# Scan inputs built by TensorE instead of VectorE in a two-layer attention, MLP, Mamba and LoRA-expert kernel

## The chip, the cores and the metric

The kernel runs on one NeuronCore of a Trainium2 chip. The metric is the device time of one execution in microseconds (us). Before the change it is 840.49 us, the median of 3 runs (839.77 to 840.96).

## The reference

The input is x of 4 sequences by 256 tokens by 512 channels, in float32. Layer 0 adds a latent attention and a gated MLP to x; the change doesn't touch it. Layer 1 adds a selective scan (Mamba) and a mixture of low-rank experts on a dense base. Cut to what matters here, for each sequence:

```python
proj = xn @ in_proj_w                       # 512 -> 2 x 1024
x, z = split(proj)                          # both [1024, 256]
xc = silu(conv_b + sum_k conv_w[:, k] * shift(x, k))        # 4 taps
ssm = xc.T @ x_proj_w.T                     # 32 + 16 + 16 columns
dt_r, B, C = rmsnorm of the three parts
dt = softplus(dt_r @ dt_proj_w.T + dt_bias)                 # [1024, 256]
h[d, n, t] = exp(dt[d, t] * A[d, n]) * h[d, n, t-1] + dt[d, t] * B[n, t] * xc[d, t]
ys[d, t] = sum over the 16 n of h[d, n, t] * C[n, t]
y = (ys + D * xc) * silu(z)
out = y.T @ out_proj_w.T  (+ x + the experts)
```

The recurrence runs over 256 times for 4 sequences x 1024 channels d x 16 states n.

## The kernel before, in words

All work is written out by hand in program order for five engines; nothing is scheduled by a planner. Layer 0 comes first, with the last blocks of its MLP (`ff`, the generator `down`) trickling into the beginning of layer 1.

Layer 1 is a loop over 128 units `u` (L1377), 32 for each sequence: `b` is the sequence, `c` one of 8 blocks of 128 channels, `g` one of 4 groups of states. A tile of a unit has 128 partitions = 4 states x 32 channels, and a free dimension of 4 channel quarters x 256 times, 1024 in all. For each unit:

- `decays` (L969), ScalarE: four exponentials of 255 columns give exp(dt*A). It runs two units ahead.
- `scan_in` (L983), VectorE: one multiplication of 1024 columns, `bx` = a row of B (`brow`, in PSUM) times `dus`, where `dus` is dt*x laid out over 32-channel quarters. It writes PSUM, one buffer of two banks.
- `scan` (L991): VectorE's scan instruction over 1024 columns gives `h`; then GpSimd multiplies it by the row of C into `hc`.
- `states_sum` (L1012), TensorE: four float32 matmuls with 32 output columns each, one for each quarter of the output partitions, add `hc` into `ysum`. At a block's first unit a matmul with a diagonal of D (`dgs`, L1016) opens the sum.

To get from 128 channels in partitions to 32 channels x 4 states, dt and dt*x are written to DRAM (`send`, L931) and read back four times over (`spread`, L935), for each block, by SyncE's queue. `take_sum` (L1021) and `gate` (L1025) close a block, and `out_mm` (L1113) projects it.

Around these, a table (`put` and its kin, L1241 to L1373) places the other work at certain units: the input projections `px_mm` and `pz_mm`, the convolution (`conv_in`, `conv_taps`), `pp_mm` to `pp_norm`, the step sizes, and the dense and expert parts. Softplus is taken apart into Abs, Relu, Exp, two Identity and Ln on ScalarE (`step_in`, `step_exp`) and three GpSimd additions (`step_out`). Silu of z runs in several sessions a sequence (`gate_silu`, L951), each with a load of an activation table before and after. [...]3 for `psmm`, which nearly every matmul group draws on, 2 for `bx`, 1 for `ysum`, 2 for `brow`.

Of the kernel before, what the change touches and what calls it, by code (L numbers as in the profile page):

```python
# [8 lines left out]
F32 = mybir.dt.float32  # L9
# [8 lines left out]
P = 128  # L18
# [10 lines left out]
NG = 4  # L29
# [12 lines left out]
def block_kernel(  # L42
# [604 lines left out]
    psx = ctx.enter_context(tc.tile_pool(name="psx", bufs=1, space=PSUM))  # L647
    psy = ctx.enter_context(tc.tile_pool(name="psy", bufs=1, space=PSUM))
    psb = ctx.enter_context(tc.tile_pool(name="psb", bufs=1, space=PSUM))
# [6 lines left out]
    xcs, nrms, dts, szs, crows = {}, {}, {}, {}, {}  # L656


    al = w1.tile([P, NG, DC, NST], F32, tag="u", name="al")

    def load_rest():
# [14 lines left out]
    bcsel = w1.tile([64, 2, NU, P], F32, name="bcsel")  # L676
    nc.vector.tensor_copy(
        bcsel.rearrange("p k g (n j) -> p (k g n) j", n=NG),
        ident[0:64, RK : RK + 2 * NST].unsqueeze(2).to_broadcast([64, 2 * NST, NB]),
    )  # L680
    nc.vector.tensor_reduce(stack, ident.rearrange("p (n j) -> p j n", n=NG), AX.X, ALU.add)
    dgs = w1.tile([P, DC, P], F32, name="dgs")
# [17 lines left out]
    brow = [psb.tile([P, 2, S], F32, name=f"brow{i}") for i in range(2)]  # L700
# [15 lines left out]
    def norm_stats(b):  # L716
        mv = w1.tile([P, 2, 2], F32, tag="mv1", name="mv1", bufs=2)
        for i in range(2):
            st = w1.tile([P, 6], F32, tag="st1", name="st1", bufs=2)
            nc.vector.bn_stats(st, x[:, 2 * b + i, :])  # L720
            nc.vector.bn_aggr(mv[:, i, :], st)
        rs = w1.tile([P, 2], F32, tag="rsn", name="rsn", bufs=2)
        inv_root(rs, mv[:, :, 1], eps[:, 0:1])
        live["ln", b] = mv, rs

    def norm_scale(b):
        mv, rs = live["ln", b]
        sh = w1.tile([P, 2], F32, tag="sh1", name="sh1", bufs=2)
        nc.vector.scalar_tensor_tensor(sh, mv[:, :, 0], -1.0, rs, ALU.mult, ALU.mult)
        out = []  # L730
        for i in range(2):
            t = w1.tile([P, D], F32, tag="xnt", name="xnt", bufs=2)
            nc.scalar.activation(t, x[:, 2 * b + i, :], AF.Identity, bias=sh[:, i : i + 1],
                                 scale=rs[:, i : i + 1])
            out.append(t)
# [25 lines left out]
    both = ((1, 0), (1, 3), (2, 1), (2, 3), (3, 1), (3, 3))  # L761

    def conv_in(b, p):
# [5 lines left out]
        nc.scalar.copy(pads[p % 2][:, :, KC - 1 :], px)  # L769
        v = [vec[:, 2 * p + i, :] for i in range(2)]  # L770
        if b:
            dg = live["dg"] = w1.tile([P, KC, P], F32, tag="dg", name="dg")
            for k in range(KC):
                nc.scalar.activation(dg[:, k, :], ident, AF.Identity, scale=v[0][:, V_CW + k : V_CW + k + 1])
        tp = live["tap"] = w1.tile([P, KC - 1, S], F32, tag="tap", name="tap")
        if (b, p) in both:
            tp = tp.rearrange("p k t -> p (k t)")
            for k in range(KC):
                nc.scalar.activation(tp[:, k * P : (k + 1) * P], ident, AF.Identity,
                                     scale=v[1][:, V_CW + k : V_CW + k + 1])  # L780
        else:
            nc.scalar.activation(xcs[b][:, 2 * p + 1, :], px[:, 1, :], AF.Identity,
                                 bias=v[1][:, V_CB : V_CB + 1], scale=v[1][:, V_CW + KC - 1 : V_CW + KC])
            for k in range(KC - 1):
                nc.scalar.activation(tp[:, k, :], pads[p % 2][:, 1, k : k + S], AF.Identity,
                                     scale=v[1][:, V_CW + k : V_CW + k + 1])
        if b == 0:
            nc.scalar.activation(px[:, 0, :], px[:, 0, :], AF.Identity, bias=v[0][:, V_CB : V_CB + 1],
                                 scale=v[0][:, V_CW + KC - 1 : V_CW + KC])

    def conv_taps(b, p):
        px, c = live["px", b, p], 2 * p
        if b == 0:
            for k in range(KC - 1):
                nc.vector.scalar_tensor_tensor(
                    px[:, 0, :] if k < KC - 2 else xcs[b][:, c, :], pads[p % 2][:, 0, k : k + S],
                    vec[:, c, V_CW + k : V_CW + k + 1], px[:, 0, :], ALU.mult, ALU.add,
                )
        else:

            for i in range(1 + ((b, p) in both)):
                for k in range(KC):
                    dg = live["tap"].rearrange("p k t -> p (k t)")[:, k * P : (k + 1) * P]
                    mm(px[:, i, :], lhsT=dg if i else live["dg"][:, k, :],  # L804
                       rhs=pads[p % 2][:, i, k : k + S], start=(k == 0), stop=(k == KC - 1))
            if p < NP - 1:
                conv_out(b, p)
        if (b, p) not in both:
            xc = xcs[b][:, c + 1, :]
            for k in range(KC - 1):  # L810
                nc.gpsimd.tensor_tensor(xc, xc, live["tap"][:, k, :], ALU.add)

    def conv_out(b, p):
        for i in range(1 + ((b, p) in both)):
            c = 2 * p + i
            nc.scalar.activation(xcs[b][:, c, :], live["px", b, p][:, i, :], AF.Identity,
                                 bias=vec[:, c, V_CB : V_CB + 1])

    def conv_silu(b, z=None):
        nc.scalar.activation(xcs[b], xcs[b], AF.Silu)  # L820
        if z is not None:
            gate_silu(*z)
        else:
            exp_set()
# [9 lines left out]
    def pp_square(b):  # L834
        pp = live["pp"]
        sq = w1.tile([64, S], F32, tag="sq", name="sq")
        nc.scalar.activation(sq, pp[:64, 0, :], AF.Square)
        mm(pp[:64, 1, :], lhsT=cst[:64, C_BLK : C_BLK + 64], rhs=sq, start=True, stop=True)
        live["rs"] = w1.tile([64, S], F32, tag="sq", name="rs1")
# [9 lines left out]
    def b_rows(b, i):  # L849

        for g in (2 * i, 2 * i + 1):
            mm(brow[i][:, g % 2, :], lhsT=bcsel[:, 0, g, :], rhs=nrms[b], start=True, stop=True)

    def c_rows(b, i):
        pc = psmm.tile([P, 2, S], F32, tag="mm", name="pcr")
        for j in range(2):
            mm(pc[:, j, :], lhsT=bcsel[:, 1, 2 * i + j, :], rhs=nrms[b], start=True, stop=True)
# [5 lines left out]
    def step_in(b, h, q, part=(0, 1)):  # L863
        if q == 0 and part[0] == 0:
            dts[b, h] = odd(h).tile([P, HALF, S], F32, tag="dt", name="dt")
            live["u"] = w1.tile([P, HALF, S], F32, tag="u", name="u")
        pd = psmm.tile([P, 2, S], F32, tag="mm", name="pdt")
        for i in part:
            c = h * HALF + 2 * q + i
            mm(pd[:, i, :], lhsT=dtw[:, c * P : (c + 1) * P], rhs=nrms[b][0:RK, :],  # L870
               start=True, stop=True)
        for i in part:
            j = 2 * q + i
            db = vec[:, h * HALF + j, V_DB : V_DB + 1]
            nc.scalar.activation(live["u"][:, j, :], pd[:, i, :], AF.Abs, bias=db)
            nc.scalar.activation(dts[b, h][:, j, :], pd[:, i, :], AF.Relu, bias=db)

    def step_exp(b, h, q=slice(0, 4)):

        if q.start == 0:  # L880
            live["lw"] = w1.tile([P, HALF, S], F32, tag="lw", name="lw")
            live["e"] = w1.tile([P, HALF, S], F32, tag="e", name="e")
        u, w, e = (live[n][:, q, :] for n in ("u", "lw", "e"))
        nc.scalar.activation(u, u, AF.Exp, scale=-1.0)
        nc.scalar.activation(w, u, AF.Identity, bias=1.0)
        nc.scalar.activation(e, w, AF.Identity, bias=eps[:, 2:3])
        nc.scalar.activation(w, w, AF.Ln)


    def one_step(c):  # L890
        pd = psmm.tile([P, 2, S], F32, tag="mm", name="pdt")[:, 0, :]
        mm(pd, lhsT=dtw[:, c * P : (c + 1) * P], rhs=nrms[0][0:RK, :], start=True, stop=True)
        t = live["one"] = w1.tile([P, KC - 1, S], F32, tag="tap", name="one")
        u, w, e = (t[:, k, :] for k in range(3))
        db = vec[:, c, V_DB : V_DB + 1]
        nc.scalar.activation(u, pd, AF.Abs, bias=db)
        nc.scalar.activation(dts[0, 0][:, c, :], pd, AF.Relu, bias=db)
        nc.scalar.activation(u, u, AF.Exp, scale=-1.0)
        nc.scalar.activation(w, u, AF.Identity, bias=1.0)
        nc.scalar.activation(e, w, AF.Identity, bias=eps[:, 2:3])  # L900
        nc.scalar.activation(w, w, AF.Ln)

    def one_out(c):
        u, w, e = (live["one"][:, k, :] for k in range(3))
        dt = dts[0, 0][:, c, :]
        nc.gpsimd.tensor_tensor(e, u, e, ALU.subtract)
        nc.gpsimd.tensor_tensor(e, e, w, ALU.add)
        nc.gpsimd.tensor_tensor(dt, dt, e, ALU.add)

    def step_out(b, h, q, k):  # L910
        s = slice(2 * q, 2 * q + 2)
        e, dt = live["e"][:, s, :], dts[b, h][:, s, :]
        if k == 0:
            nc.gpsimd.tensor_tensor(e, live["u"][:, s, :], e, ALU.subtract)
        elif k == 1:
            nc.gpsimd.tensor_tensor(e, e, live["lw"][:, s, :], ALU.add)
        else:
            nc.gpsimd.tensor_tensor(dt, dt, e, ALU.add)
            send("dt", b, 2 * h + q, dt)

    def step_x(b, p):

# [608 lines left out]
```

## Time and profile before

The profile is of one execution, whose span is 839.1 us; the median of the runs is 1.4 us more.

| | us |
|---|---|
| median of the runs | 840.49 |
| span of the profiled execution | 839.1 |
| first scan input (L986) starts | 327.45 |
| last scan (L1001) starts | 830.3 |
| from the one to the other (the scan stage) | 502.8 |
| busy over the whole span: TensorE, VectorE, ScalarE, GpSimd | 748.8, 655.1, 554.7, 496.7 |

A group row names line, engine and operation, then output and inputs with their shapes, the count, the busy time, the mean duration of one in ns, and the idle time of the engine just before. For a tiled matmul, `128*32` is rows by columns of the array in use. A float32 matmul appears as two MATMUL and two LDWEIGHTS records, so that the four matmuls of `states_sum` are eight of each.

### The profile page before, as it was taken

To read this page: it belongs to the slowest core of one execution; us is meant where nothing else is said; L and a number is where in the kernel's file an instruction comes from. 1 tells how busy PE (TensorE), PEld (TensorE's weight loads), DVE (VectorE), ACT (ScalarE), POOL (GpSimd) and SP (SyncE) were. 2 spreads that over 40 slices of the span, in tenths; PEclk is the share of its full clock that TensorE was granted. 3 is DMA by queue.
4 is the path that set the end of the run, shared out by engine and by line. 5 is a ranking of instruction groups with operands and counts; after the bars stand their busy time and mean duration, and the time that the engine had idled before them with its cause. 6 is when DMAs were issued, how large, how long until landed. Compare 5 with 4: busy or idle time off the path is not lost.

```text
span 839.1 us, 11113 instructions
## 1 busy us (share of the span) xinstructions
PE 748.8 (89%) x3846; PEld 429.7 (51%) x3846; DVE 655.1 (78%) x604; ACT 554.7 (66%) x1124; POOL 496.7 (59%) x389
## 2 busy tenths in 40 slices
PE   4999999999999999999887899888999987956885
PEld 2665545666555676666543457444457444312331
DVE  4486756288634435798899999989999989999996
ACT  4335564435556277699896898687898786865561
POOL 3133332001343333688869799769699769798764
PEclk9799999999999999999999999989999989998998
DMA  7233332001222332554593554443553343343400
GB/s 226 63 101 105 97 101 62 1 1 38 76 76 80 114 57 64 151 140 125 137 215 114 150 155 125 110 103 117 144 164 114 88 113 111 103 125 102 113 26 25
DMA packets 68642, 86.71 MB, mean 103 GB/s; under 512 B 12221, under 2 KB 52169, under 8 KB 68458
## 3 DMA queue, kind: packets, MB, share of 16 engines
q1 hardware_dynamic: 58794, 65.81, 29.3%
q0 software_dynamic: 9072, 18.35, 7.9%
q10 hardware_dynamic: 720, 1.84, 0.6%
q8 instruction: 30, 0.49, 0.2%
q14 instruction: 26, 0.21, 0.1%
HBM read 66.58 MB, written 10.22 MB: 92 GB/s over the span
## 4 chain that ended last, share of the span: by engine, by line
PE 51%; DVE 25%; ACT 15%; POOL 5%; issue 3%; DMA 1%; DVEq 0%; POOLq 0%; ACTq 0%; SPq 0%
DVE h L1001 15%; ACT decay L980 7%; PE pg L444 6%; PE pu L444 5%; PE po L469 5%; PE px L757 4%; DVE bx L986 4%; POOL hc L1006 4%; PE av L397 4%; PE px L804 4%; PE ysum L1018 3%; PE scT L386 2%; DVE mpl L354 2%; PE pp L831 2%; PE po L1114 2%
## 5 line engine op out<-in xcount | busy, mean ns | idle before, releaser
L1006 POOL TENSOR_TENSOR hc<-h,cr 128x1024 f32<-128x1024 f32 (+1 forms) x130 | 301.7, 2323 | 79.9 <-DVE h L1001 67.5
L1001 DVE TENSOR_TENSOR_SCAN h<-decay,bx 128x1024 f32<-128x1024 f32 (+1 forms) x129 | 288.2, 2236 | 27.0 <-POOL hc L1006 4.7
L980 ACT ACTIVATE decay<-dts,aneg 128x255 f32<-128x255 f32 x504 | 213.4, 501 | 52.3 <-DVE h L1001 42.2
L986 DVE TENSOR_TENSOR bx<-brow,dus 128x1024 f32<-128x1024 f32 x128 | 157.7, 1232 | 5.0 <-DMA dus<-dud 0.6
L1018 PE MATMUL ysum<-hc,stack 128*32 128x256 f32 x1024 | 89.6, 419 | 42.2 <-POOL hc L1006 41.9
L456 POOL TENSOR_TENSOR hlo<-g,hhi 128x512 fp32r<-128x512 f32 x28 | 35.8, 1280 | 115.0 <-ACT hhi L455 115.0
L354 DVE TENSOR_REDUCE mpl<-sc 128x4 f32<-128x1024 f32 x64 | 76.7, 1219 | 22.8 <-PE sc L352 21.3
L427 POOL DMA_DIRECT2D wgu<-in_wgu x56 | 31.1, 555 | 95.9 <-PE pg L444 94.7
L388 ACT ACTIVATE pe<-scT 128x1024 f32<-128x1024 f32 x64 | 64.0, 1023 | 22.9 <-PE sc L352 14.3
L1114 PE MATMUL po<-ow,xc 128*128 128x512 f32 x128 | 69.4, 646 | 4.3 <-POOL xc L1026 3.9
L1018 PEld LDWEIGHTS ysum<-hc,stack 128*32 128x32 f32 x1024 | 21.3, 111 | 100.3 <-POOL hc L1006 70.6
L948 PE MATMUL pz<-xn1T,w_in 128*128 128x256 f32 x256 | 69.4, 420 | 0.0
L948 PEld LDWEIGHTS pz<-xn1T,w_in 128*128 128x128 f32 x256 | 50.8, 208 | 20.7 <-issue 11.9
L757 PE MATMUL px<-xn1T,w_in 128*128 128x256 f32 x256 | 60.9, 383 | 0.4 <-ACT sz L954 0.3
L757 PEld LDWEIGHTS px<-xn1T,w_in 128*128 128x128 f32 x256 | 47.6, 190 | 13.0 <-issue 2.5
L452 DVE SCALAR_TENSOR_TENSOR g<-g,pg 128x512 f32<-128x512 f32 x28 | 19.2, 686 | 43.1 <-ACT g L451 43.1
L444 PE MATMUL pg<-xhi,wgu 128*128 128x512 f32 x112 | 49.6, 443 | 1.0 <-ACT xhi L244 1.0
L469 PE MATMUL po<-wd,hhi 128*128 128x512 f32 x112 | 49.2, 439 | 0.0
L444 PE MATMUL pu<-xhi,wgu 128*128 128x512 f32 x112 | 47.6, 425 | 0.8 <-DVE g L454 0.8
L455 ACT CAST hhi<-g 128x512 fp32r<-128x512 f32 x28 | 17.3, 619 | 45.8 <-DVE g L454 45.8
L444 PE MATMUL pg<-xlo,wgu 128*128 128x512 f32 x112 | 44.9, 401 | 0.7 <-DVE xlo L251 0.7
L444 PE MATMUL pu<-xlo,wgu 128*128 128x512 f32 x112 | 44.5, 397 | 0.0
(237 smaller groups left out, 1276.8 us busy)
## 6 DMA issues: line engine op xcount, KB each, us to landing
dts<-dtd SPq DMA_DIRECT2D x124, 128.0 KB, 2.8
dus<-dud SPq DMA_DIRECT2D x124, 128.0 KB, 3.2
wgu<-in_wgu POOLq DMA_DIRECT2D x56, 256.0 KB, 2.7
w_in<-in_inz SPq DMA_DIRECT2D x16, 512.0 KB, 4.9
w_in<-in_inx SPq DMA_DIRECT2D x14, 512.0 KB, 4.3
dtd<-dt SPq DMA_DIRECT2D x15, 256.0 KB, 2.2
dud<-du SPq DMA_DIRECT2D x15, 256.0 KB, 2.2
wd<-in_wd POOLq DMA_DIRECT2D x7, 512.0 KB, 3.6
```

Of the source, the lines that this page charges most:

```text
L354: nc.vector.tensor_reduce(mpl2[b % 2][:, qb, 2 * hp : 2 * hp + 2, 16 + 2 * gq : 18 + 2 * gq], sc.rearrange("p i (f k) -> p i f k", f=2), A ...
L388: nc.scalar.activation(pes[b, k][:, 2 * t : 2 * t + 2, :], sc, AF.Exp)
L444: mm(ps, lhsT=wgus[i][:, hc, :], rhs=xs[j][:, hc, :], start=(hc == 0 and j == 0), stop=(hc == HC - 1 and j == 1))
L469: mm(po, lhsT=hids[th][j][:, m, i * P : (i + 1) * P], rhs=wd[:, m, :], start=False, stop=(m == MC - 1 and j == 1))
L757: mm(px[:, i, :], lhsT=w[:, i, hc, :], rhs=xns[b][:, hc, :], start=(hc == 0), stop=(hc == HC - 1))
L948: mm(pz[:, i, :], lhsT=w[:, i, hc, :], rhs=xns[b][:, hc, :], start=(hc == 0), stop=(hc == HC - 1))
L980: nc.scalar.activation(da[:, k, 1:], live["dts", b, c][:, k, 1:], AF.Exp, scale=aneg[:, c, k, g : g + 1])
L986: nc.vector.tensor_tensor(bx, brow[g // 2][:, g % 2, :].unsqueeze(1).to_broadcast([P, NG, S]), live["dus", b, c], ALU.mult)
L1001: nc.vector.tensor_tensor_scan(h[:, n].rearrange("p n t -> p (n t)"), da[:, n].rearrange("p n t -> p (n t)"), bx[:, n].rearrange("p n t -> ...
L1006: (nc.vector if k == NG - 1 else nc.gpsimd).tensor_tensor(hc[:, n], h[:, n], crows[b][:, g, :].unsqueeze(1).to_broadcast([P, NG // parts, ...
L1018: mm(ysum[k * NB : (k + 1) * NB, :], lhsT=stack, rhs=hc[:, k, :], start=False, stop=(g == NU - 1))
L1114: mm(live["po", b, i], lhsT=xcs[b][:, c, i * P : (i + 1) * P], rhs=late_w["ow"][:, c, :], start=False, stop=(c == DC - 1))
```

## The change

- `scan_in` is taken from VectorE and given to TensorE. `bx` becomes the product of a transposed dt*x (`dut`, made by `step_turn`) and diagonals of B (`bdg`, made by `b_turn` and `b_diag` once a sequence): 32 float32 matmuls a unit, each with 64 contraction rows, 32 output columns and 128 moving columns. `bx` gets two buffers, and the input of unit u+1 is issued at the start of unit u. The round trip of dt*x through DRAM is gone; that of dt stays.
- The order of the scans changes: a unit is now one quarter `k` of the channels with all four groups of states, so that the multiplication with C reads the whole of `crows`.
- `states_sum` sums four units at once, 16 matmuls after each fourth unit. D*x is added by VectorE in `take_sum`, and `dgs` is gone.
- Softplus is one ScalarE pass, for a whole sequence at once, between two table loads (`softplus_set`, `exp_set`). Silu of xc and z is one session a sequence (`silus`); z waits for it as a copy.
- The convolution uses other engines for some blocks: by `mode`, TensorE with diagonals that GpSimd makes once and DRAM keeps, ScalarE and GpSimd, or VectorE.
- `brow` is gone, so PSUM is 3 banks `psmm`, 4 `bx`, 1 `ysum`. One of the two accumulators `po` is closed into x and opened again by a matmul (`close_x`, `reopen`). The table of units is rewritten, and more tiles share buffers.

```diff
-    psx = ctx.enter_context(tc.tile_pool(name="psx", bufs=1, space=PSUM))
+    psx = ctx.enter_context(tc.tile_pool(name="psx", bufs=2, space=PSUM))
-    psb = ctx.enter_context(tc.tile_pool(name="psb", bufs=1, space=PSUM))
...
+    def mode(b, p, i):
+
+        if b == 0:
+            return "dve" if i == 0 else "act"
+        return "pe" if i == 0 else "act" if p < 2 else "dve"
...
+    def silus(b, z):
+
+        nc.scalar.preload_act_table_set("silu_and_others")
+        if b < B:
+            nc.scalar.activation(xcs[b], xcs[b], AF.Silu)
+        nc.scalar.activation(szs[z], szs[z], AF.Silu)
+        exp_set()
...
+    def b_turn(b):
+
+        bt = live["bt"] = psmm.tile([P, 4, 8], F32, tag="mm", name="pbt")
+        for t in range(4):
+            for r in range(2):
+                mm(bt[r * HT : (r + 1) * HT, t, :], lhsT=nrms[b][:, t * HT : (t + 1) * HT],
+                   rhs=ident[0:64, RK + 8 * r : RK + 8 * r + 8], start=True, stop=True)
+
+    def b_diag():
+
+        for i in range(2):
+            nc.vector.tensor_tensor(
+                bdg[:, 2 * i : 2 * i + 2].rearrange("p t g n j -> p (t g n) j"),
+                eye.unsqueeze(1).to_broadcast([P, NST, HT]),
+                live["bt"][:, 2 * i : 2 * i + 2, :].rearrange("p t s -> p (t s)").unsqueeze(2)
+                .to_broadcast([P, NST, HT]), ALU.mult,
+            )
...
+    def step(b, p):
...
+            nc.scalar.activation(dts[b][:, c, :], pd[:, i, :], AF.Softplus, bias=vec[:, c, V_DB : V_DB + 1])
...
+    def step_x(b, c, eng=nc.gpsimd):
+
+        live["du", c] = w1.tile([P, S], F32, tag="du", name="du", bufs=2)
+        eng.tensor_tensor(live["du", c], dts[b][:, c, :], xcs[b][:, c, :], ALU.mult)
+
+    def step_turn(b, c):
+
+        du = live["du", c]
+        pt = psmm.tile([P, 4, P], F32, tag="mm", name="ptu")
+        for t in range(4):
+            for r in range(2):
+                mm(pt[r * HT : (r + 1) * HT, t, :], lhsT=du[:, t * HT : (t + 1) * HT], rhs=ident,
+                   start=True, stop=True)
+        dut[b, c] = w1.tile([P, 4, P], F32, tag="dut", name="dut", bufs=2)
+        nc.scalar.copy(dut[b, c], pt)
...
     def scan_in(u):
-        b, c, g = u // PER, u % PER // NU, u % NU
-        bx = psx.tile([P, NG, S], F32, tag="bx", name="bx")
-        nc.vector.tensor_tensor(
-            bx, brow[g // 2][:, g % 2, :].unsqueeze(1).to_broadcast([P, NG, S]), live["dus", b, c], ALU.mult
-        )
-        live["bx"] = bx
+        b, c, k = u // PER, u % PER // NU, u % NU
+        bx = live["bx", u] = psx.tile([P, NU, S], F32, tag="bx", name="bx")
+        for t in range(4):
+            for n in range(NG):
+                for r in range(2):
+                    w = slice(r * HT, (r + 1) * HT)
+                    mm(bx[n * NB : (n + 1) * NB, 2 * r : 2 * r + 2, t * HT : (t + 1) * HT],
+                       lhsT=dut[b, c][w, t, k * NB : (k + 1) * NB], rhs=bdg[w, t, :, n, :],
+                       start=True, stop=True)
...
-    def states_sum(u):
-        b, c, g = u // PER, u % PER // NU, u % NU
-        hc = live.pop(("hc", u))
-        if g == 0:
-            mm(ysum, lhsT=dgs[:, c, :], rhs=xcs[b][:, c, :], start=True, stop=False)
-        for k in range(NG):
-            mm(ysum[k * NB : (k + 1) * NB, :], lhsT=stack, rhs=hc[:, k, :],
-               start=False, stop=(g == NU - 1))
...
+    def states_sum(q, ks=range(NG), gs=range(NU)):
+
+        hc = [live["hc", q * NU + k] for k in range(NG)]
+        for g in gs:
+            for k in ks:
+                mm(ysum[k * NB : (k + 1) * NB, :], lhsT=stack, rhs=hc[k][:, g, :],
+                   start=(g == 0), stop=(g == NU - 1))
+
+    def take_sum(b, c, w=slice(0, S)):
+
+        nc.vector.scalar_tensor_tensor(
+            xcs[b][:, c, w], xcs[b][:, c, w], vec[:, c, V_D : V_D + 1], ysum[:, w], ALU.mult, ALU.add
+        )
...
+    def reopen(b, i):
+        live["po", b, i] = psmm.tile([P, D], F32, tag="mm", name="po2")
+        mm(live["po", b, i], lhsT=ident, rhs=x[:, 2 * b + i, :], start=True, stop=False)
...
+    for u in range(total):
+        for f, a in first_at.get(u, ()):
+            f(*a)
         if 3 <= u < total - 2:
             decays(u + 2)
-        for f, a in at.get(u, ()):
+        if u + 1 < total:
+            scan_in(u + 1)
+        for f, a in (*soon_at.get(u, ()), *at.get(u, ())):
             f(*a)
...
+        scan(u, 1 if u < total - 1 else 4)
...
+        if u >= 5 and u % NU == 1:
+            q = u // NU - 1
+            states_sum(q)
+            take_sum(q // DC, q % DC)
```

## The prediction, made before the change was run

> **What bounds the kernel now.** I read the page first for the engines' shares and the costliest groups, then VectorE's timeline for the pitch of a unit, then busy time by stretches, then TensorE's timeline for what a small tiled group costs. From the page:
>
> ```profile
> span 839.1 us, 11113 instructions
> ...
> PE 748.8 (89%) x3846; PEld 429.7 (51%) x3846; DVE 655.1 (78%) x604; ACT 554.7 (66%) x1124; POOL 496.7 (59%) x389
> ...
> L1006 POOL TENSOR_TENSOR hc<-h,cr 128x1024 f32<-128x1024 f32 (+1 forms) x130 | 301.7, 2323 | 79.9 <-DVE h L1001 67.5
> L1001 DVE TENSOR_TENSOR_SCAN h<-decay,bx 128x1024 f32<-128x1024 f32 (+1 forms) x129 | 288.2, 2236 | 27.0 <-POOL hc L1006 4.7
> ...
> L986 DVE TENSOR_TENSOR bx<-brow,dus 128x1024 f32<-128x1024 f32 x128 | 157.7, 1232 | 5.0 <-DMA dus<-dud 0.6
> ```
>
> The scan idles 27 us in 128 units: VectorE seldom waits. Its timeline in the middle sequence:
>
> ```profile
> 481.79 2.29 DVE L1001 TENSOR_TENSOR_SCAN h<-decay,bx 128x1024 f32<-128x1024 f32 x1
> 484.11 1.23 DVE L986 TENSOR_TENSOR bx<-brow,dus 128x1024 f32<-128x1024 f32 x1
> 485.47 2.29 DVE L1001 TENSOR_TENSOR_SCAN h<-decay,bx 128x1024 f32<-128x1024 f32 x1
> ```
>
> A unit takes 3.68 us (481.79 to 485.47), all of it VectorE. So VectorE sets the scan stage: 128 x 3.68 = 471 of its 502.8 us. But TensorE is close behind. Busy time in the four sequences (columns: length, then PE, PEld, DVE, ACT, POOL, the granted clock, DMA):
>
> ```profile
> 327.50:465.60 138.10, 121.03 (x654) 77.02 (x653) 122.00 (x100) 113.42 (x257) 107.93 (x71) 0.95 0.58 149
> 465.60:588.70 123.10, 112.48 (x556) 61.32 (x554) 114.58 (x71) 102.41 (x232) 104.06 (x63) 0.92 0.46 124
> 588.70:712.80 124.10, 114.13 (x595) 63.97 (x595) 117.14 (x89) 102.03 (x234) 103.13 (x61) 0.95 0.44 121
> 712.80:830.30 117.50, 87.19 (x426) 33.89 (x424) 112.09 (x67) 71.62 (x153) 91.91 (x52) 0.94 0.31 85
> ```
>
> TensorE is busy 121.0 + 112.5 + 114.1 + 87.2 = 434.8 us of 502.8. The change takes 1.23 us a unit from VectorE and hands the work to the engine with 68 us left. The price of a tiled group decides, and TensorE's timeline shows one between two plain groups:
>
> ```profile
> 570.13 1.99 PE L948 MATMUL pz<-xn1T,w_in 128*128 128x256 f32 x8
> 572.05 0.64 PE L1018 MATMUL ysum<-hc,stack 128*32 128x256 f32 x8
> 572.62 1.99 PE L948 MATMUL pz<-xn1T,w_in 128*128 128x256 f32 x8
> ```
>
> Undisturbed, eight passes of 256 columns take 1.73 us (the chain of waits has many such pieces, as px at 502.31), 0.216 us a pass. Here the first group needs 1.92 us to the next start, 0.19 more, and `ysum` 0.57: together 0.76. The eight `ysum` passes ran on four column tiles at once: two passes of streaming, 0.43. The other 0.33 us is the price of entering and leaving the tiled mode.
>
> [...]
>
> **The change part by part**, in TensorE time of the scan stage:
>
> - `bx`: 32 matmuls are 64 passes of 128 columns. At half of 0.216, 0.108 each, on eight tiles: 8 x 0.108 = 0.86 us. Plus 0.33 for the mode and 0.06 for staggered starts (`ysum` starts about 7 ns apart): 1.25 us, x128 = +160. Unknown: never below 0.86; above, see the rivals.
> - `step_turn`: 8 matmuls of 128 columns on two column tiles, 16 / 2 x 0.108 + 0.33 = 1.19, x32 = +38. `b_turn` and `reopen`: 4 x 0.8 + 3 x 0.9 = +6.
> - `states_sum`: 128 x 0.76 = 97 becomes 32 x (8 x 0.216 + 0.33) = 66: -31.
> - `dgs` -14 (64 passes x 0.216), `brow` -6 (26 x 0.216), convolution -10 (144 passes become 96).
>
> Sum +143: 434.8 + 143 = 578. Busy time overstates occupation, because the last pass before each gap is drawn 0.16 us too long (a pass of 0.216 as 0.38), about 100 times, 16 us. [...]That leaves 548 us of work for a stage of 502.8.
>
> Moved off at no gain, because TensorE's 548 covers it: VectorE 466 - 158 + 15 (`take_sum`, 32 x 0.48) + 10 (`b_diag`, 8 x 1.23) + 9 (convolution taps, 18 x 0.49) = 342. GpSimd: `hc` 128 x 2.36 = 302, gates 23, `step_x` 31 x 0.73 = 23, taps 18 x 0.73 = 13, diagonals 4 x 1.27 = 5: 366, the next bound. ScalarE 389 - 46 (softplus one pass of 32 x 0.47 for 61 us in six rows) - 8 (fewer table loads of 1.28) - 23 (diagonals of the convolution) - 11 (`take_sum`) + 19 (copies of `ptu`, 32 x 0.58) + 12 (copies of pz): 332. The trace has no Softplus pass; between the 0.47 us of Abs (L875) and double that, it stays hidden. Without TensorE's cover these three would show: GpSimd first, at 366. On SyncE's queue 124 spreads of dt*x and their 15 writes go, and eight 256 KB loads of diagonals come; the trace has 0.6 us of waits for `dus`, so nothing is won there now.
>
> Waits: [...]A group that waits for a `psmm` buffer holds up the next `bx`, and VectorE's scan with it. Groups that need one of the three buffers rise from about 26 to 40 a sequence, with one buffer mostly held by `po`. ScalarE, which empties them, is 60% busy; I put 17 us for these waits (bounds 5 to 40). The old waits for `hc` (42 us of idle at L1018) go, since sums come a unit late.
>
> Before the stage: after `nrm` (317.6) now come dt's matmuls 0.9, eight softplus passes 3.8, a table load 1.28, the copy of `ptu` 0.58 and the first `bx` 1.25: first scan near 327 against 329.1, so -2. After the last scan much the same work follows, 8.8 us.
>
> Sum: the first `bx` near 325.5, plus 548 + 17, plus 8.8 = 899 us for the span; with the 1.4 us that the median has above the span, **900 us**, slower by 7%.
>
> **The rivals.**
>
> *Issue or tiles hold `bx` up.* [...]If the two row halves take turns, 1.71 + 0.33 = 2.04, +101, 1001 us. [...]For: nothing in the trace issues 128 short instructions in a row.[...]
>
> *Faster: TensorE is cheaper than I count.* The stage breaks even where a unit's `bx` adds no more than (505 - 17 - 388) / 128 = 0.78 us (388 is 548 without `bx`), under its pure streaming. It needs 64-row passes that cost half of mine: then 388 + 17 + 55 = 460 and 796 us, with GpSimd's 366 the floor, some 700. For: VectorE, ScalarE and GpSimd all get a quarter or more lighter, and every old bound is relieved. Against: pass time follows columns alone in every row that I read.
>
> *No change*: those errors happen to cancel, at `bx` near 0.78 us; 840.
>
> **How the numbers follow.** TensorE-bound with eight tiles at work, 845 to 930: 0.66, the likeliest, 900. Held up by issue or tiles, 930 to 1020: 0.19. Faster: 0.13, about 796. Within 0.2%, which is about what a measurement of this kernel can tell from no change: 0.02. The range 848 to 985 leaves out the faster case, and the far part of the slow one: it takes in about 0.78. The bounds within the main case: without switching and waits, 548 - 192 x 0.33 + 5 = 490 would even win, but the 0.33 is in every group that I read, so 848 is the low end.
>
> **What would show it.** Right: scans at a pitch over 4 us, idle before L1001's scan put down to TensorE's `bx`; TensorE over 95% busy with a clock near 1.0; eight `bx` passes starting together; VectorE and GpSimd under 70%. `bx` groups near 1.25 us from start to next start confirm the main term; over 2 us, the first rival. Wrong: scans back to back near 2.4 to 3 us, or TensorE idle for `psmm` buffers by more than 40 us.

## The result and the profile after

The changed kernel takes 917.33 us, the median of 4 runs (915.16 to 919.74), against 840.13 us (838.08 to 840.96, 4 runs) for the kernel before on the same chip: the ratio is 1.0921, 95% interval 1.0897 to 1.0946. It is slower by 9%; forecast were 900 us and 7%. The profiled execution has a span of 915.9 us.

The page of the changed kernel, engines and groups:

```profile
span 915.9 us, 27817 instructions
...
PE 860.5 (94%) x12468; PEld 556.3 (61%) x12468; DVE 530.8 (58%) x530; ACT 498.8 (54%) x985; POOL 443.9 (48%) x349
...
L1000 POOL TENSOR_TENSOR hc<-h,cr 128x1024 f32<-128x1024 f32 (+1 forms) x130 | 302.3, 2333 | 221.3 <-PE ysum L1009 138.8
L995 DVE TENSOR_TENSOR_SCAN h<-decay,bx 128x1024 f32<-128x1024 f32 (+1 forms) x129 | 284.1, 2226 | 51.9 <-PE bx L977 36.6
L977 PE MATMUL bx<-bdg,dut 64*32 64x128 f32 x8192 | 149.1, 276 | 19.5 <-DVE h L995 10.3
...
L1014 DVE SCALAR_TENSOR_TENSOR xc<-xc,vec,ysum 128x256 f32<-128x256 f32 (+1 forms) x33 | 15.6, 472 | 146.8 <-PE ysum L1009 146.8
```

VectorE is 124 us less busy than before (655.1 there), ScalarE 56 and GpSimd 53 less; TensorE is 112 us busier. The wait ahead of the scan now names TensorE's `bx`. The largest wait, 146.8 us for `ysum`, looks like the cause; moving it gained nothing, as the experiments show.

Busy time by sequence (columns as in the prediction: length, PE, PEld, DVE, ACT, POOL, the granted clock, DMA):

```profile
329.40:485.80 156.40, 147.60 (x2776) 104.63 (x2775) 92.32 (x79) 92.79 (x206) 91.96 (x59) 0.98 0.36 103
485.80:631.10 145.30, 138.63 (x2720) 91.18 (x2719) 84.51 (x55) 88.66 (x193) 90.74 (x55) 0.98 0.27 78
631.10:779.50 148.40, 142.09 (x2756) 94.81 (x2757) 88.01 (x77) 89.89 (x198) 90.47 (x55) 0.98 0.26 73
779.50:904.40 124.90, 114.80 (x2568) 70.25 (x2568) 76.69 (x44) 62.08 (x141) 84.71 (x48) 0.97 0.14 41
```

TensorE is busy 543.1 of 575 us at a clock of 0.97 to 0.98; before it was 434.8 of 502.8 at 0.92 to 0.95. VectorE, which filled its stage before, is now busy for 59%. TensorE's timeline, with the same kind of neighbours as in the prediction:

```profile
564.26 1.16 PE L977 MATMUL bx<-bdg,dut 64*32 64x128 f32 x64
565.35 1.09 PE L920 MATMUL ptu<-cst,du 128*64 128x128 f32 x16
566.38 1.99 PE L759 MATMUL px<-xn1T,w_in 128*128 128x256 f32 x8
568.30 1.16 PE L977 MATMUL bx<-bdg,dut 64*32 64x128 f32 x64
569.39 2.00 PE L815 MATMUL pc<-pad,dg 128*128 128x256 f32 x8
```

A `bx` group takes 1.09 us from its start to the next start (564.26 to 565.35; 568.30 to 569.39). The plain group between two tiled ones needs 1.92 us (566.38 to 568.30) where 1.73 is usual. About half of these 0.19 us goes with each tiled neighbour, and a `bx` group between plain groups has two such neighbours, so it costs 1.09 + 0.19 = 1.28 us a unit.

The chain of waits says the same in one column (start, us, what): in this piece it leaves TensorE only for the copy of `dut`.

```profile
495.77 1.86 PE ysum L1009 x32
497.63 1.09 PE bx L977 x64
498.72 1.91 PE po L1112 x4
500.63 1.73 PE pz L942 x8
502.36 1.05 PE ptu L920 x16
503.41 0.02 issue
503.43 0.59 ACT dut L923
```

### The profile page after: what moved, and what is told of

The parts are those of the page before. It is cut to its first block, busy times and chain, and to the rows that moved or that the text cites. A ratio compares the mean times of both kernels' runs of the same rounds, so it can differ in the third digit from the quotient of the medians.

```text
span 915.9 us, 27817 instructions
## 1 busy us (share of the span) xinstructions
PE 860.5 (94%) x12468; PEld 556.3 (61%) x12468; DVE 530.8 (58%) x530; ACT 498.8 (54%) x985; POOL 443.9 (48%) x349
## 4 chain that ended last, share of the span: by engine, by line
PE 40%; ACT 4%; DVE 4%; POOL 3%; issue 1%; POOLq 0%; ACTq 0%; DVEq 0%
PE bx L977 9%; PE ysum L1009 6%; PE po L1112 5%; PE pz L942 5%; PE px L759 3%; PE po L1096 3%; DVE h L995 3%; PE ptu L920 3%; POOL hc L1000 2%; ACT decay L967 2%; PE pc L815 1%; PE pp L845 1%; DVE bdg L874 1%; PE pcr L884 1%; PE pdt L900 1%
## 5 line engine op out<-in xcount | busy, mean ns | idle before, releaser
L1000 POOL TENSOR_TENSOR hc<-h,cr 128x1024 f32<-128x1024 f32 (+1 forms) x130 | 302.3, 2333 | 221.3 <-PE ysum L1009 138.8
L995 DVE TENSOR_TENSOR_SCAN h<-decay,bx 128x1024 f32<-128x1024 f32 (+1 forms) x129 | 284.1, 2226 | 51.9 <-PE bx L977 36.6
L977 PE MATMUL bx<-bdg,dut 64*32 64x128 f32 x8192 | 149.1, 276 | 19.5 <-DVE h L995 10.3
L977 PEld LDWEIGHTS bx<-bdg,dut 64*32 64x32 f32 x8192 | 115.2, 106 | 73.9 <-issue 37.1
L1014 DVE SCALAR_TENSOR_TENSOR xc<-xc,vec,ysum 128x256 f32<-128x256 f32 (+1 forms) x33 | 15.6, 472 | 146.8 <-PE ysum L1009 146.8
L1112 PE MATMUL po<-ow,xc 128*128 128x512 f32 x128 | 63.9, 619 | 2.8 <-POOL xc L1019 2.1
L1009 PE MATMUL ysum<-hc,stack 128*32 128x256 f32 x1024 | 66.5, 396 | 0.1
L923 ACT COPY dut<-ptu 128x512 f32<-128x512 f32 x32 | 18.7, 583 | 81.4 <-PE ptu L920 81.4
L942 PE MATMUL pz<-xn1T,w_in 128*128 128x256 f32 x256 | 62.7, 388 | 0.0
L942 PEld LDWEIGHTS pz<-xn1T,w_in 128*128 128x128 f32 x256 | 46.9, 190 | 14.4 <-issue 9.4
L1009 PEld LDWEIGHTS ysum<-hc,stack 128*32 128x32 f32 x1024 | 31.7, 113 | 32.6 <-issue 15.1
```

The lines of the kernel that those rows point to most:

```text
L942: mm(pz, lhsT=w[:, c % 2, hc, :], rhs=xns[b][:, hc, :], start=(hc == 0), stop=(hc == HC - 1))
L977: mm(bx[n * NB : (n + 1) * NB, 2 * r : 2 * r + 2, t * HT : (t + 1) * HT], lhsT=dut[b, c][w, t, k * NB : (k + 1) * NB], rhs=bdg[w, t, :, n, :],
L995: nc.vector.tensor_tensor_scan(h[:, n].rearrange("p n t -> p (n t)"), da[:, n].rearrange("p n t -> p (n t)"), bx[:, n].rearrange("p n t -> ...
L1000: (nc.vector if i == NG - 1 else nc.gpsimd).tensor_tensor(hc[:, n], h[:, n], crows[b][:, n, :], ALU.mult,)
L1009: mm(ysum[k * NB : (k + 1) * NB, :], lhsT=stack, rhs=hc[k][:, g, :], start=(g == 0), stop=(g == NU - 1))
L1112: mm(live["po", b, i], lhsT=xcs[b][:, c, i * P : (i + 1) * P], rhs=late_w["ow"][:, c, :], start=False, stop=(c == DC - 1))
```

## The experiments

The theory to test: TensorE sets the time of the changed kernel, and `bx` is what put it over. The rivals: the wait for the sums, or the other parts of the change, hold it up. Where the stage is given below, it runs from the first scan's start to the last scan's start.

**Half-precision scan inputs.** `bdg` and `dut` are rounded to float16; the trace of this run then has 32 passes in a `bx` group instead of 64.

```diff
-    bdg = w1.tile([P, 4, 2, NG, HT], F32, name="bdg")
+    bdg = w1.tile([P, 4, 2, NG, HT], F16, name="bdg")
-        dut[b, c] = w1.tile([P, 4, P], F32, tag="dut", ...)
+        dut[b, c] = w1.tile([P, 4, P], F16, tag="dut", ...)
```

> The changed kernel with the operands of the scan-input matmuls (the turned dt*x and the diagonals of B) rounded to float16; everything else as in the change. The computation is the same but for that rounding. A float16 matmul is one pass where float32 is two, and a pass of 128 columns streams in 0.053 us where a float32 pass takes 0.107, so a unit's group loses 8 x 0.107 - 4 x 0.053 = 0.64 us of its 1.09. TensorE-bound (my theory): 128 x 0.64 = 82 us go from 917, 835 to 845 us, with the pitch of the scans near 3.7 us. If the waits for buffers and not TensorE's work set the pace: over 880 us.[...]

Measured: 865.22 us (863.88 to 866.34), ratio to before 1.0291 (1.0257 to 1.0325). In TensorE's timeline a group is now 0.35 us to the next start, and a round of eight passes starts 0.055 us after the last one (in float32 0.109; the expectation had 0.053 and 0.107):

```profile
542.02 0.42 PE L977 MATMUL bx<-bdg,dut 64*32 64x128 f16 x32
542.37 1.09 PE L920 MATMUL ptu<-cst,du 128*64 128x128 f32 x16
```

TensorE's busy time in the stage falls by 78 us (540.0 to 462.0), the run by 52, to more than the 835 to 845 us expected. So `bx` in float32 on TensorE costs at least 52 us; but the gain stops 25 us above the kernel before, and TensorE has 57 us of gaps in its stage of 519 us. Something else of the change holds it there.

**More work on either engine.** The z projection's matmuls are issued twice, in the kernel after and in the kernel before: 256 more passes of 0.216, 55 us on TensorE. And in the kernel after, odd units scan twice: 64 x 2.28 = 146 us on VectorE.

```diff
-        for hc in range(HC):
+        for hc in [*range(HC), *range(HC)]:
             mm(pz, lhsT=w[:, c % 2, hc, :], ...
...
-            nc.vector.tensor_tensor_scan(...)
+            for _ in range(1 + u % 2):
+                nc.vector.tensor_tensor_scan(...)
```

> The changed kernel with every z projection computed twice, the second time over the first: 32 groups x 1.73 = 55 us more work for TensorE and nothing for the others. TensorE-bound: 965 to 975 us. If its 32 us of idle in the scan stage could take work up: down to 940. If it is not the bound: under 930 us.

> The kernel before with every z projection computed twice, 32 groups x 1.73 = 55 us more for TensorE, as in the run of the changed kernel, which rose by 54 us. In the kernel before TensorE is idle 70 us of the scan stage and VectorE sets the pace: 845 to 865 us, most of the 55 taken up. If TensorE is the bound there already: 890 us or more.

> The changed kernel with the scan instruction issued twice in every odd unit, the second writing the same values again: 64 x 2.28 = 146 us more work for VectorE, nothing more for TensorE. TensorE-bound: VectorE's 345 us in the scan stage become 491, still under TensorE's 543 busy, so 917 to 935 us. If VectorE's chain of scans is still on the path: up to 1060 us.

Measured, with one execution each: z twice 971.76 us after (+54.4) and 861.0 before (+20.6), both as expected; the scan twice 960.94 (+44), more than the 917 to 935 expected. The same 55 us cost the changed kernel all of it and the kernel before two fifths. Of 146 us of VectorE work, the changed kernel absorbs 100. The other 44 show in TensorE's stage as 24 us more of gaps and 19 us more of busy time, at a granted clock of 0.95 instead of 0.98. TensorE sets its time; VectorE has slack, though not in every unit.

**Later sums.** `take_sum`, which has the 146.8 us wait, is moved one unit back.

```diff
         if u >= 5 and u % NU == 1:
             q = u // NU - 1
             states_sum(q)
+        if u >= 6 and u % NU == 2:
+            q = u // NU - 1
             take_sum(q // DC, q % DC)
...
-            put_late(b, max(4 * c + 5, last + 1 + c), gate, b, c)
+            put_late(b, max(4 * c + 6, last + 1 + c), gate, b, c)
```

> The changed kernel with VectorE's reading of the sum (take_sum, and the gate behind it) one unit later, so that the scan of the next unit stands ahead of it in VectorE's queue. The computation is the same. VectorE waited 147 us for the sums in the changed kernel. If TensorE's work sets the time, that wait was VectorE's slack: 905 to 917 us, the wait is found elsewhere (scans waiting for their inputs). If the wait holds up the scans and so the next inputs: 880 to 900 us.

> Scan inputs from float16 operands, as before, and the sum taken one unit later. With float16 alone 865 us came instead of 840: TensorE's busy time in the scan stage fell by 78 us, the time by 52. If VectorE's wait for the sums, with the next scan behind it, is what held the rest: 840 to 852 us. If the waits for buffers or for ScalarE's copies are: 860 to 867 us.

Measured: 923.75 us (ratio 1.1000, 1.0945 to 1.1055), and on the half-precision kernel 867.67 (1.0324, 1.0280 to 1.0368). Nothing is gained by either; both lie a little above the ranges expected for slack. In the changed kernel's stage VectorE's wait for the sums falls from 143.7 to 49.9 us, but its scans now wait 67.3 us for `bx` instead of 36.6, and 48.8 us for GpSimd's `hc` instead of 11.2; its idle time is 229 us against 232. So VectorE's largest wait was mostly time in which it would have waited for something else. GpSimd waits for the same sums too, since they hold `hc` buffers; the edit leaves that wait as it was (140.1 us, 138.8 before the edit), so it isn't tested here.

**Scan inputs back on VectorE.** All of the change is kept except the place of `bx`: VectorE multiplies `brow` by `dus` again, dt*x goes through DRAM again, and PSUM is 3 banks `psmm`, 2 `bx`, 2 `brow`, 1 `ysum`. The new order of units makes `dus` a quarter of the channels and `brow` all 16 states.

```diff
-        for t in range(4):
-            for n in range(NG):
-                for r in range(2):
-                    ... mm(bx[...], lhsT=dut[b, c][...], rhs=bdg[...])
+        nc.vector.tensor_tensor(
+            bx, brow, dut[b, c][:, k, :].unsqueeze(1).to_broadcast([P, NU, S]), ALU.mult)
...
-        if u + 1 < total:
-            scan_in(u + 1)
+        if u:
+            scan_in(u)
```

> The changed kernel with the scan inputs given back to VectorE (rows of B in PSUM times dt*x that goes through DRAM, one buffer); the one-pass softplus, the one silu session, the sums of four units, D*x on VectorE, the other convolution and the rewritten table stay. The computation is the same. My theory: all of the loss is the scan inputs, so VectorE sets the pace again at 3.68 us a unit, plus 16 us for the sums with D and 9 us for taps: 840 to 860 us. If the rest of the change (the table, the buffers, the sessions) costs too: 870 us or more. If the relief of ScalarE and GpSimd was worth something: under 835 us.

> Scan inputs on VectorE, as before, and the sum taken one unit later. In the run without this VectorE was busy 496 us of the scan stage's 567 and waited for the sums 27 us, in front of the next scan. If those waits are real losses where VectorE sets the pace: 875 to 885 us, and the remainder over 840 is its 31 us of added work. If they only stand for another wait: 900 to 910 us.

Measured: 909.47 us (ratio 1.0825, 1.0793 to 1.0857), and with the later sums 908.91 (1.0814, 1.0766 to 1.0861). The expectation missed: the rest of the change costs 69 us with the scan inputs on VectorE, and this kernel is only 8 us faster than the changed one. VectorE is busy 496 of 567 us in the stage, 31 more than in the kernel before; new there are the convolution's taps (20.8) and `take_sum` (14.4). Its waits make up the other half. With the later sums its wait for them falls from 26.8 to 5.1 us, and that for the spreads of dt*x rises from 8.5 to 17.9. Most units keep a pitch of 3.7 us, but at much the same units of the first three sequences it breaks. One such place in the timeline:

```profile
593.41 2.29 DVE L978 TENSOR_TENSOR_SCAN h<-decay,bx 128x1024 f32<-128x1024 f32 x1
...
595.90 1.57 ACT L893 ACTIVATE dt<-pdt,vec 128x256 f32<-128x256 f32 x4 [4.75 <-POOL du L901]
596.79 3.77 PE L889 MATMUL pdt<-nrm,dtw 32*128 32x256 f32 x8 [1.95 <-ACT dt L893]
...
600.50 3.36 PE L992 MATMUL ysum<-hc,stack 128*32 128x256 f32 x32
...
604.01 0.48 DVE L997 SCALAR_TENSOR_TENSOR xc<-xc,vec,ysum 128x256 f32<-128x256 f32 x1 [8.31 <-PE ysum L992]
...
605.77 2.29 DVE L978 TENSOR_TENSOR_SCAN h<-decay,bx 128x1024 f32<-128x1024 f32 x1
```

The pitch is 12.4 us. Softplus of the next sequence waits 4.75 us until GpSimd's `du` has read the old `dt` for the last time; TensorE's `pdt` waits for Softplus; the sums stand behind `pdt` in TensorE's queue; and VectorE's `take_sum`, ahead of the next scan, waits 8.31 us for them.

**Two waits less.** The last `step_x` of a sequence goes two units earlier, so that `dt` comes free sooner, and the six blocks with taps on VectorE take them on ScalarE and GpSimd. It is done to the kernel with `bx` on VectorE and to the changed kernel.

```diff
-        return "pe" if i == 0 else "act" if p < 2 else "dve"
+        return "pe" if i == 0 else "act"
...
-            put_late(b, 4 * c - 4, step_x, b, c)
+            put_late(b, 4 * c - 4 - 2 * (c == DC - 1), step_x, b, c)
```

> Scan inputs on VectorE, as in the first such run (909 us), with two edits against waits that its trace shows: the convolution taps that stood on VectorE (3.5 us a block, 6 blocks) go to ScalarE and GpSimd, and the last dt*x of a sequence is made two units earlier, so that Softplus, which writes the same buffer, doesn't wait for it (4.7 us a sequence on ScalarE, with TensorE and then VectorE behind it). The computation is the same. If these waits are what the rest of the change costs: 6 x 3.5 + 3 x 5 = 36 us less, 870 to 885 us. If each is only one of several that end together: 895 us or more.

> The changed kernel, scan inputs on TensorE, with the same two edits. Here TensorE's work sets the time and VectorE has slack, so the taps cost nothing; only the wait of Softplus, which stops TensorE too, can give something: 905 to 915 us. If VectorE's stalls matter here as well: 880 to 895 us.

Measured: 891.07 us (ratio 1.0611, 1.0569 to 1.0652), 18 less, half of what was expected; and 906.09 (1.0784, 1.0745 to 1.0823) for the changed kernel, 11 less, as expected. In the first, the stage is 18.8 us shorter and VectorE's busy time in it 19.3 (496.1 to 476.7), while its idle time stays (71.3 and 71.8). So the gain is the taps, VectorE's own work. Softplus no longer waits for `du`, but VectorE's wait for the sums rose from 26.8 to 33.1 us. One place of it, in the timeline:

```profile
566.71 3.12 PE L848 MATMUL pp<-xc,xpw 128*64 128x256 f32 x8 [4.66 <-ACT xc L839]
...
569.76 2.38 PE L992 MATMUL ysum<-hc,stack 128*32 128x256 f32 x32
...
572.22 2.36 POOL L983 TENSOR_TENSOR hc<-h,cr 128x1024 f32<-128x1024 f32 x1 [4.50 <-PE ysum L992]
572.30 0.48 DVE L997 SCALAR_TENSOR_TENSOR xc<-xc,vec,ysum 128x256 f32<-128x256 f32 x1 [5.00 <-PE ysum L992]
```

Another group that waits, `pp` for the silu session, stands ahead of the sums. GpSimd waits beside VectorE, since the sums of four units hold `hc` buffers.

**Sums first.** In the same kernel, `states_sum` is issued at the start of its unit, ahead of the groups that the table places there.

```diff
+        if u >= 5 and u % NU == 1:
+            states_sum(u // NU - 1)
         for f, a in (*soon_at.get(u, ()), *at.get(u, ())):
             f(*a)
...
-            states_sum(q)
             take_sum(q // DC, q % DC)
```

> The kernel with scan inputs on VectorE and the two waits less (891 us), with one more edit: the four-unit sum is issued on TensorE at the start of its unit, ahead of the groups that the table places in that unit, and no longer behind them. VectorE's additions of D*x, which wait for it, stay where they are. In the run before, VectorE waited 33.1 us for these sums, up to 5.7 us at a time, and at two of the places that I read, a group stood ahead of the sum that waited itself: the convolution for its diagonals, the projection pp for the silu session. If the order in TensorE's queue is the cause: 855 to 872 us, and that wait falls under 12 us. If it is slack that stands for another wait (the last unit's product with C comes late anyway, or a decay, or a spread is next): 885 to 895. If TensorE now stands still ahead of the input projection and loses the time elsewhere: over 895.

Measured: 873.42 us (872.3 to 874.7), ratio 1.0403 (1.0364 to 1.0442): another 18 us less, 1.4 above the range expected. VectorE's waits, first with two waits less:

```profile
DVE xc L997 <- PE ysum L992: 33.1, 13, 5.7
DVE bx L960 <- DMA dus<-dud: 9.8, 7, 3.0
```

then with the sums first:

```profile
DVE bx L960 <- DMA dus<-dud: 21.5, 11, 4.7
...
DVE xc L997 <- PE ysum L992: 4.8, 4, 2.2
```

The wait for sums goes from 33.1 to 4.8 us, and GpSimd's for the same sums from 37.1 to 2.3, so the order in TensorE's queue was the cause there. About 12 us come back as waits for the spreads of dt*x, which took 0.6 in the kernel before. Of the 34 us that remain to the kernel before, the stage has 30 (530.8 against 501.2): 10 of VectorE's work (474.7 against 464.6) and 21 of this wait would account for it. No run took the latter away.

**Less work on TensorE.** To the changed kernel: the half-precision scan inputs, `du` and the identity of `step_turn` in float16, `hc` and `stack` of the sums in float16, the two waits less, and three pieces of the MLP drawn forward, one ahead of each later pair of the first sequence's step sizes.

```diff
-        live["du", c] = w1.tile([P, S], F32, tag="du", ...)
+        live["du", c] = w1.tile([P, S], F16, tag="du", ...)
-               lhsT=du[:, t * HT : (t + 1) * HT], rhs=ident,
+               lhsT=du[:, t * HT : (t + 1) * HT], rhs=idf,
-        return act.tile([P, NG, S], F32, tag="hc", ...)
+        return act.tile([P, NG, S], F16, tag="hc", ...)
...
     for p in range(1, NP):
+        go(ff, 1)
         step(0, p)
```

> The changed kernel with all tiled work of TensorE from float16 operands: scan inputs, the turning of dt*x, and the sums (GpSimd writes h*C as float16); the two edits against waits[...]. Only roundings differ. TensorE's 462 us in the stage with float16 inputs alone lose 32 x 0.64 = 20 for the turns and 32 x 1.28 = 41 for the sums, 400 us. If TensorE's work still sets the time, 865 - 61 - 5 = 800 us; with the part of each saving that came through before, two thirds, 815 to 830 us, faster than the kernel before. If the table's waits (ScalarE's sessions, buffers) set the time from 865 on: 845 us or more.

Measured: 816.21 us (815.44 to 822.02), ratio 0.9727 (0.9688 to 0.9766): faster than both kernels, and within the 815 to 830 expected.

```profile
span 814.2 us, 18101 instructions
...
PE 725.3 (89%) x7604; PEld 443.5 (54%) x7604; DVE 518.4 (64%) x514; ACT 503.0 (62%) x1003; POOL 454.5 (56%) x367
```

TensorE is 135 us less busy than in the changed kernel, and the median is 101 us lower. The change pays once what VectorE gives up costs TensorE less than its free time; the price is scan inputs and sums rounded to float16. The run makes these edits together, and apart from the scan inputs (52 us) and the two waits (11) their shares weren't measured.

## Why the prediction was right, and where it was off

*The bound moves to TensorE*: right. Of the prediction's signs these appeared: a mean scan pitch of (904.4 - 332.5) / 127 = 4.5 us, idle time before the scan put down to `bx` (36.6 of 51.9 us), eight `bx` passes starting within 0.05 us, VectorE and GpSimd under 70% (58% and 48%), the clock near 1.0 (0.97 to 0.98). TensorE is 94% busy, not over 95%. The pair with z twice shows that it sets the end.

*The price of `bx`, 1.25 us*: right, 1.28 measured. The first rival falls. The weight loads of a group, 64 of them, all within 0.89 us, together with 64 passes:

```profile
490.97 0.89 PEld L977 LDWEIGHTS bx<-bdg,dut 64*32 64x32 f32 x64 [0.76 <-DVE st L722]
490.97 1.16 PE L977 MATMUL bx<-bdg,dut 64*32 64x128 f32 x64
```

128 instructions in 1.09 us are 8.5 ns each; in this rival's 930 to 1020 us the cost of issue was the author's estimate, which no trace showed. And 64 passes of 0.108 (in the kernel before, passes of 128, 256 and 512 columns start 0.109, 0.216 and 0.429 us apart), one after another, would be 6.9 us, and with the two row halves in turns 1.71: the eight tiles work together. The prediction assumed that; the trace before has no tiles of 64 rows by 32 columns. `step_turn` took 1.03 to 1.05 us and the four-unit sum 1.86 to the next start; with 0.19 for plain neighbours, which the predicted 1.19 and 2.06 include, that is 1.23 and 2.05.

*548 us of work on TensorE*: 543 from the first `bx` to the last scan, but this closeness is partly luck. The prediction took 16 us off the busy time for about 100 gaps before which a pass is drawn 0.16 us too long (its own sum, 578 - 16 - 15, is 547; the 15, for a higher granted clock, was the author's estimate). The trace of the kernel before has 56 gaps in its stage, that of the changed kernel 28. With 0.16 us for each of the 28, an estimate, the changed kernel has 539 us of work, 9 less than forecast, and 36 of gaps, 19 more. The forecast busy times of the other engines hold: 342, 332 and 366 us for VectorE, ScalarE and GpSimd, against 341.5, 333.4 and 357.9.

*The miss is 17 us*: about 4 at the start, 15 in the gaps and 3 in the tail, less 5 of work, all from busy time as it is drawn.

- The first `bx` starts at 329.35 us, not near 325.5, and the first scan at 332.5, not near 327. The prediction's own terms end that `bx` at 325.4, so it counted this group twice. It gave dt's matmuls 0.9 us, which is the first four passes at 0.216, and let the other twelve run beside Softplus. In the timeline those twelve are the longest piece:

```profile
318.68 5.48 PE L900 MATMUL pdt<-nrm,dtw 32*128 32x256 f32 x12 [0.93 <-ACT dt L904]
324.10 1.98 PE L920 MATMUL ptu<-cst,du 128*64 128x128 f32 x16
326.00 3.42 PE L1188 MATMUL pdts<-dt,dg 128*128 128x256 f32 x8
329.35 1.16 PE L977 MATMUL bx<-bdg,dut 64*32 64x128 f32 x64
...
330.78 1.70 ACT L967 ACTIVATE decay<-dts,aneg 128x255 f32<-128x255 f32 x4 [3.84 <-DVE dts L1190]
332.51 2.29 DVE L995 TENSOR_TENSOR_SCAN h<-decay,bx 128x1024 f32<-128x1024 f32 x1 [1.83 <-ACT decay L967]
```

  The twelve passes of `pdt` take 5.48 us with no wait between them, where 0.216 a pass would be 2.6: the granted clock is 0.50 from 318.7 to 326.0 us and 0.56 from there to 329.35, where the kernel before had 1.00. Softplus waits for these passes, not they for it. `ptu` then takes 1.90 us to the next start instead of 1.03, and `pdts`, the first spread of dt by TensorE, 3.35 instead of 1.73 for eight passes, at the same clock. The prediction's sum left `pdts` out, and with it VectorE's copy of it and the first decays (330.78 to 332.48), which the first scan waits for in place of `bx`.

- TensorE's gaps in the stage are 32 us (575 - 543), not 17, though within the bounds of 5 to 40. The waits of `bx` itself are for `h`, which frees a `bx` buffer (10.3), and for `dut` (9.1). Groups that write a `psmm` buffer and wait for the engine that empties one (`pdt`, `ptu`, `pt`) have 7.8 us: the mechanism that the prediction named is there, but it is the smaller part.
- The tail after the last scan's start is 11.5 us, not 8.8.

*The rest of the change moves off at no gain*: right for the changed kernel, but the faster rival took it as relief, and it isn't. By that rival's sum, with `bx` under 0.78 us a unit the stage should break even. Half precision brought `bx` to 0.35 + 0.19 = 0.54 us, for which that sum gives 325.5 + 388 + 128 x 0.54 + 17 + 8.8 = 808 us; the span was 864.6. The step that failed is the constant 17 us of waits: TensorE's gaps were 57 us there, 40 of the 56 that the sum lacks. The largest of them are waits of `bx` for the scan (25.7) and for `dut` (11.3); what is behind these isn't shown. With `bx` on VectorE, runs took out 36 us of what the rest of the change costs: 18 with the taps, which are VectorE's own work, and 18 with the sums that stood behind groups that wait. In the changed kernel two of the three edits gave 11 us; the third wasn't tried there. The costs don't add: against the kernel before, all of the change but its `bx` is 8% slower with `bx` on VectorE, 3% with `bx` in half precision on TensorE, and 9% with `bx` in float32 there.

## What to carry to other kernels

Price moved work on the engine that receives it, what a tiled group costs its plain neighbours included (0.19 of 1.28 us here), against that engine's idle time in that stage; then ask the same of the second-longest chain, since it sets the time as soon as the first is mended. A long wait in the list isn't yet a cost: letting VectorE take the sums later gained nothing, in the version with 147 us of waits for them and in one with 27, but making the sums themselves earlier gained 18 us in a version with 33. Compare busy and idle time of the stage before and after an edit, too: an edit meant against waits gained 18 us by taking work from VectorE. With the sums issued ahead of the table's groups, VectorE's wait for them fell from 33.1 to 4.8 us: a short group that others wait for belongs ahead of long groups that wait themselves.

## What the runs showed of the hardware that was not expected

- TensorE took 64 weight loads and 64 passes on tiles of 64 rows by 32 columns in 1.086 us (the median distance of 107 groups), 8 x 0.108 = 0.86 of it streaming. The rest of the price, 0.19 us, falls on the plain neighbours: eight passes of 256 columns take 1.73 us between plain groups, 1.82 with a tiled group behind them, 1.83 with one ahead, and 1.92 with one on either side.
- VectorE's convolution tap has a median of 0.485 us, but 5 of the 27 take 1.15 to 2.48, and 6 more 0.83 to 0.87. In the timeline the three taps of one block take 3.52 us, beside GpSimd's product with C:

```profile
567.28 4.94 POOL L1000 TENSOR_TENSOR hc<-h,cr 128x1024 f32<-128x1024 f32 x2 [0.52 <-DVE h L995]
569.50 3.52 DVE L820 SCALAR_TENSOR_TENSOR xc<-pad,vec,xc 128x256 f32<-128x256 f32 x3 [0.19 <-ACT xc L798]
```

  These 11 taps all start inside a GpSimd instruction, at least 0.55 us before its end, and end 0.28 us after it: the tap of 2.48 us starts at 570.02, inside a product that ends at 572.22. The 15 taps that start outside one take 0.48 to 0.49. Why a tap lasts that long then isn't shown. `take_sum`, the same instruction with one input in PSUM, takes 0.48 us at most in the 30 places where it lies inside such a product. The 11 taps are 8 us over the median together in the changed kernel. With `bx` on VectorE the second tap of each of the six blocks takes 2.45 to 2.48 us, 12 us over the median together, which is most of what taking the taps off VectorE gained there.
